# Another order of the sixteen column transfers of a band: 0, 4, 8, 12, 1, ... in place of 0, 8, 1, 9, ...

## The chip, the core and the metric

The kernel runs on one core of a Trainium2 chip. The core has TensorE (PE, matmuls, with its weight loads PEld), VectorE (DVE), ScalarE (ACT), GpSimd (POOL) and SyncE (SP), and 16 DMA engines that move data between HBM and the on-chip memory SBUF. POOL and SP issue the DMAs here. The metric is the device time of one execution in microseconds; less is better.

## The reference

Two layers on x of shape 32 x 256 x 32 x 32, float32.

```python
# layer 0: 3x3 convolution of the group-normalised x, with rounding to a 16-bit format
x = x + conv3x3_quantized(_gn(x), weight, bias)
# layer 1: involution of the group-normalised x
xn = _gn(x)
y = relu(bn(einsum('oc,bchw->bohw', w1, xn)))             # 256 -> 64 channels
w = einsum('oc,bchw->bohw', w2, y) + b2                   # 16 groups x 49 taps for each pixel
w = w.reshape(b, G, K * K, H, W)
patches = ...                                             # the 7x7 surroundings of each pixel of xn
x = x + einsum('bgkhw,bgckhw->bgchw', w, patches)         # each pixel has its own 7x7 filter per group
```

In layer 1 each pixel of each image has 16 x 49 weights of its own, worked out from the image, and the sum over its 7 x 7 surroundings uses them.

## The kernel before, in words

Images are worked through one after another, in a schedule written out by hand: a loop over steps n (line 549), 16 steps to an image (`per`, line 540). At each step every stage is asked, with its own lag, what is due (`due`, line 542), and issues it. The order of the code in the loop is the order of each engine's queue.

For an image, `front` (line 284) normalises, runs the convolution (line 332, TensorE), adds it to x, normalises again, makes y (line 380) and transposes the pixels (line 395). `weights` (line 402) makes the filter weights of four rows with matmuls (line 410) and VectorE puts them, with b2, into a ring `w_sb` (line 428).

The filters then have to change their place. A pixel's contributions go to its 7 x 7 surroundings, and the kernel does that sum as a matmul in which the contracted partitions are pixels. `scatter` (line 466) writes the ring to HBM, to the tensor `wd` of 32 rows x 38 columns x 1124 float32, with seven SP transfers for a band of eight image rows (line 477), in packets of 640 bytes. `load_bands` (line 479) reads the band back into SBUF, to one of three band tiles of 128 partitions x 2 sides x 3524 float32. Partition 16 r + j of a band holds row r (of 8) and column j (of 16) of each of the two sides of the image. Four bands make an image, 128 the whole run.

A band is loaded by sixteen transfers, one for each column j. Each goes to eight partitions (j, j + 16, ..., j + 112), for each of the two sides, with rows of 1124 float32 (4496 bytes): 16 such rows, 70.2 KB. In the loop over i from 0 to 15, j is worked out from i (line 483). Which queue issues it follows from i alone: i = 7 and i = 15 go to SP, the other fourteen to POOL (line 489). Inside one partition column j begins at j x 160 float32, so the transfers write disjoint places.

`sums` (line 501) multiplies the band with the pixels (line 515): each matmul takes 64 partitions, that is four rows with all sixteen columns. `add_windows` (line 523) adds the result to x with VectorE (line 531), and `store` (line 533) writes x to the output from SP. `load_bands` of a band is due 9 steps ahead of its `sums` (line 590).

The semaphores that the program uses let eight POOL transfers be out at once: each waits for the POOL transfer eight places before it. The first transfer of a band on each queue also waits for the scatters that wrote its rows of `wd` and for the matmuls that last read that band tile.

Of the kernel before, what the change touches and what calls it, by code (L numbers as in the profile page):

```python
# [41 lines left out]
JC = W // SIDES  # L42
# [29 lines left out]
def tile_quant_conv_then_involution(  # L72
# [406 lines left out]
    def load_bands(b, k):  # L479

        band = bands[(b * K + k) % NBAND]
        for i in range(JC):
            j = i // 2 + i % 2 * JC // 2
            src = bass.AP(
                tensor=wd.tensor,
                offset=wd.offset + k * TR * ROW + (j + PAD1) * WPIX,
                ap=[[ROW - 1, TR], [JC * WPIX, SIDES], [1, WPIX]],
            )
            queue = nc.sync if i % SHARE == SHARE - 1 else nc.gpsimd
            queue.dma_start(band[j::JC, :, j * WB : j * WB + WPIX], src)  # L490
# [51 lines left out]
    def due(n, lag):  # L542

        b, i = divmod(n - lag, per)
        return (b, i) if 0 <= b < B else (None, None)

    with tc.manual_schedule():
        fronts = {}
        for n in range(FRONT, B * per + 2):
            b, i = due(n, FRONT)  # L550
# [12 lines left out]
            b, i = due(n, 0)  # L563
            if b is not None and i % 2 == 0:
                sums(b, i // 2)
            b, i = due(n, 1)
# [6 lines left out]
            b, i = due(n, 2)  # L573
            if b is not None and i == 2 * (M - 1 - SIDES):
                store(b, 0)
            b, i = due(n, -LEAD)
# [3 lines left out]
            for part in range(2):  # L580
                b, i = due(n, -LEAD + 1 + part)
# [4 lines left out]
            b, i = due(n, LOAD)  # L586
# [3 lines left out]
            b, i = due(n, 3 - 4 * NBAND)  # L590
            if b is not None and i % 4 == 0:
                load_bands(b, i // 4)
# [37 lines left out]
```

## Time and profile before

| | |
|---|---|
| runs | 1381.25, 1392.44, 1393.82 us; median 1392.44 |
| span of the profiled execution, first to last instruction | 1387.9 us (its own time isn't recorded beside it; the median of the runs is 4.5 us more) |
| mean granted clock of TensorE | 0.981 |
| VectorE, ScalarE, POOL busy | 934.7, 727.6, 1007.6 us |
| POOL transfers of line 490 | 1792, 547 ns each to issue |
| SP transfers of line 490 | 256, 602 ns each to issue (median) |
| HBM read, written | 183.81 MB, 180.74 MB: 263 GB/s over the span |

How to read a profile here: an engine's busy time says how full it is, not whether it sets the end. A line such as `X L1 <- Y L2: a, n, m` in the waits says that X stood idle before line L1 for a us in all, n times, at most m us, and that Y's line L2 was the last to release it. The chain of work that ended last is followed back from the last instruction, at each step to what released it. DMA queue q0 is POOL's, q1 is SP's; their shares are the time of their packets over 16 engines' span.

### The profile page before, as it was taken

The page shows a single profiled execution, that of the slowest core. Times are in us where ns is not written, and L with a number is a line of the kernel's source. Part 1 is how long each engine was busy: PE and PEld are TensorE (multiplying, and loading weights), DVE is VectorE, ACT ScalarE, POOL GpSimd, SP SyncE. Part 2 cuts the span into 40 slices and gives each one's busy share as a digit, 9 for nine tenths or more (in the row PEclk, how much of TensorE's full clock was granted, in tenths as well). Part 3 has the DMA queues.
Part 4 walks back from the last instruction along what each step waited for, and adds up shares of the span by engine and source line. Part 5 has one row for each costly group of instructions (what it writes and reads, how often), then busy time and mean ns, then how long its engine had stood idle before and what let it go on. Part 6 is the DMA issues. An engine that isn't in the chain of part 4 may idle for free.

```text
span 1387.9 us, 70012 instructions
## 1 busy us (share of the span) xinstructions
PE 1250.5 (90%) x29440; PEld 798.5 (58%) x29440; DVE 934.7 (67%) x3179; ACT 727.6 (52%) x1699; POOL 1007.6 (73%) x1818
## 2 busy tenths in 40 slices
PE   2899999899899999998899999899999999999665
PEld 1356555566565665655565666566566655666543
DVE  4467776677767776776576677667777776677652
ACT  4866555465645555655455555545565654653300
POOL 8057777777787777767777787776876777778785
PEclk9999999999999999999999999999999999999986
DMA  6079999999999998999999999999999999999995
GB/s 217 1 195 286 283 277 283 284 266 292 287 277 274 287 294 254 285 279 269 273 275 286 289 275 279 288 277 264 288 283 272 295 285 279 280 280 272 280 269 162
DMA packets 366232, 369.33 MB, mean 266 GB/s; under 512 B 78624, under 2 KB 308192, under 8 KB 365664
## 3 DMA queue, kind: packets, MB, share of 16 engines
q1 hardware_dynamic: 279904, 235.72, 57.5%
q0 software_dynamic: 86016, 129.14, 33.8%
q8 instruction: 234, 3.83, 1.2%
q14 instruction: 78, 0.64, 0.1%
HBM read 183.81 MB, written 180.74 MB: 263 GB/s over the span
## 4 chain that ended last, share of the span: by engine, by line
PE 55%; DMA 25%; DVE 5%; issue 5%; POOL 4%; SPq 3%; ACT 3%; POOLq 0%; DVEq 0%; ACTq 0%
PE pc L332 22%; PE acc L515 17%; DMA band<-wd 14%; PE pw L410 10%; DMA wd<-w_sb 8%; POOL band L490 4%; PE py L380 3%; DVE w_sb L428 3%; SPq L477 3%; PE pt L395 2%; DMA out<-x 1%; ACT junk L219 1%; DVE x L531 1%; DMA band<-in_w 1%; ACT xn L278 0%
## 5 line engine op out<-in xcount | busy, mean ns | idle before, releaser
L490 POOL DMA_DIRECT2D band<-wd x1792 | 978.0, 548 | 364.1 <-DMA band<-wd 225.3
L428 DVE TENSOR_TENSOR w_sb<-pw,b_sb 128x16 f32<-128x16 f32 (+9 forms) x1920 | 455.5, 349 | 359.2 <-PE pw L410 345.4
L332 PE MATMUL pc<-xq,wq 128*128 128x496 f16 (+3 forms) x2304 | 536.4, 379 | 32.5 <-ACT xq L278 28.0
L515 PE MATMUL acc<-band,pixels 64*32 64x190 f32 (+1 forms) x16384 | 411.6, 322 | 80.2 <-DMA band<-wd 44.6
L332 PEld LDWEIGHTS <-wq 128*128 128x128 f16 x2304 | 206.8, 98 | 328.2 <-issue 113.0
L515 PEld LDWEIGHTS acc<-band,pixels 64*32 64x32 f32 x16384 | 296.1, 108 | 165.1 <-issue 100.1
L410 PE MATMUL pw<-w_sb,y 64*32 64x224 f32 (+1 forms) x8192 | 291.2, 332 | 15.1 <-issue 13.9
L531 DVE TENSOR_TENSOR x<-acc,x 128x380 f32<-128x380 f32 (+1 forms) x512 | 261.7, 511 | 33.6 <-PE acc L515 24.6
L410 PEld LDWEIGHTS pw<-w_sb,y 64*32 64x32 f32 x8192 | 180.6, 106 | 45.7 <-issue 28.8
L399 ACT COPY pixels<-pt 128x512 f32<-128x512 f32 x128 | 73.6, 575 | 224.0 <-PE pt L395 224.0
L219 ACT ACTIVATE junk<-x 128x512 f16<-128x512 f32 (+1 forms) x192 | 146.5, 763 | 18.0 <-DVE x L348 9.6
L219 ACT ACTIVATE junk<-x,mean 128x1024 f16<-128x1024 f32 x128 | 147.1, 1149 | 4.3
L250 ACT ACTIVATE s<-back,eps 128x2 f32<-128x2 f32 x64 | 18.9, 296 | 207.3 <-DVE back L235 207.2
L346 DVE TENSOR_SCALAR q<-pc 128x512 f16<-128x512 f32 x128 | 87.2, 682 | 19.2 <-PE pc L332 19.0
L278 ACT ACTIVATE xn<-x,off,rstd 128x512 f32<-128x512 f32 x128 | 96.1, 800 | 0.0
L348 DVE SCALAR_TENSOR_TENSOR x<-q,bias_sb,x 128x512 f32<-128x512 f16 x128 | 92.0, 719 | 0.2
L395 PEld LDWEIGHTS pt<-ident,xn 128*128 128x128 f32 x512 | 63.9, 142 | 27.7 <-issue 3.3
L395 PE MATMUL pt<-ident,xn 128*128 128x128 f32 x512 | 78.0, 275 | 1.5 <-ACT pixels L399 1.5
L240 ACT ACTIVATE mean<-back 128x2 f32<-128x2 f32 x64 | 12.7, 198 | 120.6 <-DVE back L235 120.6
L278 ACT ACTIVATE xq<-x,off,rstd 128x1024 f16<-128x1024 f32 x64 | 75.5, 1226 | 0.0
L380 PEld LDWEIGHTS py<-xn,w_sb 128*64 128x64 f32 x2048 | 62.7, 138 | 16.7 <-issue 8.3
L380 PE MATMUL py<-xn,w_sb 128*64 128x64 f32 x2048 | 67.5, 224 | 2.8 <-ACT xn L278 1.8
(40 smaller groups left out, 374.5 us busy)
## 6 DMA issues: line engine op xcount, KB each, us to landing
wd<-w_sb SPq DMA_DIRECT2D x896, 160.0 KB
band<-wd POOLq DMA_DIRECT2D x1792, 70.2 KB, 4.9
x<-in_x SPq DMA_DIRECT2D x64, 512.0 KB
out<-x SPq DMA_DIRECT2D x64, 512.0 KB
band<-wd SPq DMA_DIRECT2D x256, 70.2 KB
band<-in_w SPq DMA_DIRECT2D x2, 1152.0 KB
w_sb<-in_w SPq DMA_DIRECT2D x2, 196.0 KB
wd<-band SPq DMA_DIRECT2D x2, 180.0 KB
```

The source lines that it names most:

```text
L219: nc.scalar.activation(junk[:, n0:n1], src[:, h, n0:n1], func, bias=bias, accum_out=self.sums[:, i : i + 1])
L278: nc.scalar.activation(dst, src, AF.Identity, bias=self.off[:, one], scale=self.rstd[:, one])
L332: nc.tensor.matmul(pc.rearrange("p (r c) -> p r c", c=W)[:, r0 - nt * RT : r1 - nt * RT, c0:c1], wq[:, kh, k, mh * P : (mh + 1) * P], xq[: ...
L346: nc.vector.tensor_scalar(q, pc, F16_MAX, -F16_MAX, ALU.min, ALU.max)
L348: nc.vector.scalar_tensor_tensor(xt[:, mh, cols], q, bias_sb[:, mh : mh + 1], xt[:, mh, cols], ALU.add, ALU.add)
L380: nc.tensor.matmul(py[i * CR : (i + 1) * CR, cols], w1_sb[:, kh, :], px[:, r : r + 2], start=kh == 0, stop=kh == CH - 1,)
L395: nc.tensor.transpose(pt[:, i, h * P : (h + 1) * P], xn[:, h, (m + i) * P : (m + i + 1) * P], ident)
L410: nc.tensor.matmul(pws[i][t * TW : (t + 1) * TW, r, : dj.stop - dj.start], y_sb[b % 2][half, (r0 // 2 + r) * W : (r0 // 2 + r + 1) * W], w ...
L428: nc.vector.tensor_tensor(to, pws[i][:p, r : r + rows, e, d0 * G : d1 * G].rearrange("p r (d g) -> p r d g", g=G), b2_sb[:p, e, d0 * G : d ...
L490: queue.dma_start(band[j::JC, :, j * WB : j * WB + WPIX], src)
L515: nc.tensor.matmul(at[t * TW : (t + 1) * TW, h, :, f - top : l - top], px[p, a, v * GC : v * GC + TW], of[:, :, 2 * a + v, f - top : l - top],
L531: nc.vector.tensor_tensor(x_at, of, x_at, ALU.add)
```

## The change

In `load_bands` the column that is loaded at place i of the loop is another one. Before, the columns come in the order 0, 8, 1, 9, 2, 10, 3, 11, 4, 12, 5, 13, 6, 14, 7, 15. After, in the order 0, 4, 8, 12, 1, 5, 9, 13, 2, 6, 10, 14, 3, 7, 11, 15. The two that SP issues (i = 7 and 15) are columns 11 and 15 before and columns 13 and 15 after.

```diff
         band = bands[(b * K + k) % NBAND]
         for i in range(JC):
-            j = i // 2 + i % 2 * JC // 2
+            j = i % 4 * JC // 4 + i // 4
             src = bass.AP(
                 tensor=wd.tensor,
                 offset=wd.offset + k * TR * ROW + (j + PAD1) * WPIX,
```

## Prediction

> **What bounds the kernel now.** I read the page first: engine shares, queues, chain. Then five stretches of the steady part, then the waits, then what line 490 waits for.
>
> ```profile
> PE 1250.5 (90%) x29440; PEld 798.5 (58%) x29440; DVE 934.7 (67%) x3179; ACT 727.6 (52%) x1699; POOL 1007.6 (73%) x1818
> q1 hardware_dynamic: 279904, 235.72, 57.5%
> q0 software_dynamic: 86016, 129.14, 33.8%
> PE 55%; DMA 25%; DVE 5%; issue 5%; POOL 4%; SPq 3%; ACT 3%; POOLq 0%; DVEq 0%; ACTq 0%
> ```
>
> Two resources are nearly full: TensorE (90% of the span) and the 16 DMA engines (57.5 + 33.8 and 1.3 for instructions = 92.6%). The chain that ended last is 55% TensorE and 25% transfers. By stretches (columns: the stretch, its length, busy us of PE, PEld, DVE, ACT, POOL, each with its count, clock, DMA share, GB/s):
>
> ```profile
> 400.00:600.00 200.00, 190.66 (x4575) 122.05 (x4577) 141.41 (x482) 112.62 (x263) 151.82 (x279) 0.99 0.96 276
> 800.00:1000.00 200.00, 187.95 (x4488) 120.60 (x4487) 139.34 (x487) 112.22 (x262) 151.15 (x277) 0.99 0.97 278
> ```
>
> In the steady part TensorE is busy 94 to 95% of the time and the DMA engines 96 to 97%. A change in what one band packet costs could therefore reach the end. A change only in which packet comes first could not. The waits say how often TensorE stands for a band:
>
> ```profile
> DVE w_sb L428 <- PE pw L410: 345.4, 228, 5.9
> POOL band L490 <- DMA band<-wd: 225.3, 308, 2.9
> ...
> PE acc L515 <- DMA band<-wd: 44.6, 24, 5.6
> ```
>
> POOL stands 225.3 us, in 308 waits, for an earlier band transfer: each POOL transfer waits, by the semaphores of the program, for the POOL transfer eight before it, so eight are out at once. TensorE itself stands only 44.6 us for a band, in 24 waits (23.9 us in 17 of them between 200 and 1300 us). The transfers themselves:
>
> ```profile
> band<-wd POOLq DMA_DIRECT2D x1792, 70.2 KB, 4.9
> ...
> band<-wd SPq DMA_DIRECT2D x256, 70.2 KB
> ```
>
> [...] I call this the column's group, 0 to 3. The old order has groups 0, 2, 0, 2, 0, 2, 0, 2 and then 1, 3, 1, 3, 1, 3, 1, 3[...]. The new one has 0, 1, 2, 3 over and over. [...] The trace shows no engine numbers. [...] when SP's two are nearly alone (717.0 to 717.8 us) 5 to 8 of their packets are under way at once.
>
> **Does the trace show the groups?** I looked at the records of single packets, 4496 bytes each, 16 to a transfer. POOL's 28,672 have a median of 187 ns, a tenth percentile of 173 and a mean of 242.6; SP's 4,096 have a mean of 237. With 1 to 3 band packets under way (80 ns after a packet's start, no load of x beside it) the mean is 223 to 226 ns, with 6 to 8 it is 233 to 236, with 16 it is 286. So load costs something. The group does not, as far as I can see: SP's column 15 (group 3) takes 210 ns beside six or more POOL packets of the second half of a band (groups 1 and 3) and 279 beside those of the first half (0 and 2). SP's column 11 (group 2) takes 227 beside the first half, which has its own group, and 243 beside the second. [...] A fit of POOL's durations on same-group packets under way gives -0.6 +- 0.4 ns per packet, other groups +0.2 +- 0.4. Two reservations: I put packets to columns by their order of start, so neighbours can be confused; and the 279 comes from moments with much in flight at once, which load alone may explain.
>
> **The change, part by part.**
> 1. The value of j. It is worked out when the program is made; no instruction is added. Cost 0, with nothing needed to hide it.
> 2. Issues. Still 14 on POOL and 2 on SP for each of 128 bands, at 547 ns on POOL (1792 x 0.547 = 980 us, the 978.0 of the page) and 602 ns on SP. The queue follows i, not j, so nothing moves past anything on SP's or POOL's queue. SP's pair becomes columns 13 and 15 instead of 11 and 15. Cost 0.
> 3. Waits. The first transfer on each queue carries the waits for the scatters into wd and for the matmuls that read the band; these need all columns in either order. The limit of eight out goes by place in the queue too. No wait is added. Cost 0.
> 4. The reader. Each matmul of line 515 takes 64 partitions, four rows of all sixteen columns, so it needs the last landing of the sixteen; which column that is does not matter, and the first and the last place are columns 0 and 15 in both orders. Cost 0.
> 5. The packets. Bytes, lengths and number are the same: 147 MB in 32,768 packets, 2,048 for each of 16 engines. Only which SBUF partitions and which places of wd are touched together changes. This is the only term that can differ from zero. From below: [...] an engine would save 20 ns x 2,048 = 41 us. From above: if packets of one group met more often, see the slower rival, +25 us. I take 0, since the trace shows no dependence on the group and two bounds of either sign.
>
> The sum is 0 on a span of 1387.9 us. The median of the runs is 1392.4, that is 4.5 us more than this span, so I predict 1392 us. The three runs shown go from 1381 to 1394, so about 1% is what a measurement of this kernel can tell from no change.
>
> What covers a small cost: POOL needs 14 x 0.547 = 7.7 us for a band, and a band comes every (1374.2 - 81.5) / 128 = 10.1 us. Eight transfers out and 4.9 us to land make 0.61 us each, 8.6 us a band. Only when the median landing passes 10.1 / 14 x 8 = 5.8 us (+18%) does POOL's queue alone set the pace. If that cover is gone, sums of the next band are late first, then add_windows on VectorE and the store behind it.
>
> **Rivals.**
> *Faster[...].* For it: [...] DMA engines at 96 to 98% in the steady part, and the growth from 223 to 286 ns with the load. Against it: the same growth would come from HBM reads or the engines, the comparison by group goes the wrong way[...]. The engines would save up to 41 us, but TensorE can only give back its waits for a band: 24 us in the steady part. 1392 - 24 = 1368 us. It decides once packets get shorter by 24 / 2,048 us = 12 ns.
>
> *Slower[...].* [...] Say 2 of 7 packets go from 243 to the 286 ns seen with 16 under way: 2/7 x 43 = 12 ns, x 2,048 = 25 us on engines with 3% to spare. With no cover, 1392 + 25 = 1417 us. It decides from about 7 ns a packet (14 us, 1%). [...]
>
> *No effect because order is lost anyway.* With eight transfers out and engines shared with the scatter's 229,376 packets of 640 bytes, neighbours in the queue overlap in both orders; 1392 us too. It differs from the forecast in cause only.
>
> **How the numbers follow.** No difference of the packets, from either cause: 0.60, between 1381 and 1403 us. Faster rival: 0.15, down to 1368. Slower rival: 0.20, up to 1417. Something in wd's addresses that I can't price, slower: 0.05. So within 1%: 0.60, faster by over 1%: 0.15, slower: 0.25. The range from 1368 to 1417 takes in both bounds and leaves out less than 2 in 10; the likeliest case's own is 1381 to 1403.
>
> **What would show it.** Right: 1792 POOL issues at 547 ns, a landing near 4.9 us, q0 near 33.8%, POOL's wait for bands near 225 us, TensorE's for bands near 45. Faster rival: q0 below 33%, landing below 4.7 us, TensorE busy above 95% in the steady stretches. Slower rival: q0 above 35%, landing above 5.1 us, more of the chain on band<-wd. My forecast falls if the mean band packet changes by more than 7 to 12 ns, or if a wait of line 490 appears that was not there.

## The result, and the profile after

The changed kernel takes 1386.7 us (median of 20 runs) against 1393.9 us for the kernel before (20 runs beside it): ratio 0.9956, 95% interval 0.9935 to 0.9977. That is 0.4% faster, inside the 1% that the forecast called no difference. Run again later (e7 below) it came to 0.9984 (0.9963 to 1.0005), which does not exclude no change.

The page of the changed kernel, the lines that answer to those of before (engine shares, the two queues, the chain by engine):

```profile
PE 1259.7 (91%) x29440; PEld 798.8 (58%) x29440; DVE 928.0 (67%) x3179; ACT 728.1 (53%) x1699; POOL 1009.7 (73%) x1818
q1 hardware_dynamic: 279904, 235.72, 57.3%
q0 software_dynamic: 86016, 129.14, 33.7%
PE 65%; DMA 19%; issue 5%; POOL 4%; ACT 3%; DVE 2%; SPq 1%; POOLq 0%; DVEq 0%; ACTq 0%
```

Two of the steady stretches and the waits, as before:

```profile
400.00:600.00 200.00, 189.73 (x4532) 119.94 (x4516) 139.90 (x478) 111.91 (x258) 150.66 (x277) 1.00 0.97 281
800.00:1000.00 200.00, 192.34 (x4557) 122.21 (x4549) 143.36 (x513) 111.10 (x263) 152.62 (x281) 1.00 0.97 284
```

```profile
DVE w_sb L428 <- PE pw L410: 336.7, 228, 5.8
...
POOL band L490 <- DMA band<-wd: 216.6, 259, 3.3
...
PE acc L515 <- DMA band<-wd: 27.4, 15, 3.8
```

The shares of the two queues moved by 0.1 and 0.2 points, the DMA engines are as full as before (97% busy in both stretches, 96 and 97% before), POOL's wait fell by 9 us, and TensorE's wait for a band fell from 44.6 to 27.4 us. The last figure looks like the gain. It isn't safe: the same kernel profiled again in e7 shows 43.1 us there. The chain changed its shares too (DMA 25 to 19%), but in e7 DMA has 29%. Both differ more between two profiles of the changed kernel than between before and after. The lines of e7:

```profile
PE 51%; DMA 29%; POOL 5%; issue 5%; DVE 4%; ACT 3%; SPq 2%; POOLq 0%; DVEq 0%; ACTq 0%
```

```profile
POOL band L490 <- DMA band<-wd: 229.0, 288, 3.3
...
PE acc L515 <- DMA band<-wd: 43.1, 21, 6.2
```

Nor does the pair of profiled spans show the gain. Line 490 of each kernel, what the issues took and when the first and last started (before, then after):

```profile
L490 POOL DMA_DIRECT2D band<-wd x1792: 547/547/683, 81.5 to 1374.2; - x200
...
DMA to landing us min/median/max: 2.4/4.9/8.1
```

```profile
L490 POOL DMA_DIRECT2D band<-wd x1792: 547/547/681, 75.0 to 1371.4; - x200
...
DMA to landing us min/median/max: 2.4/4.9/8.8
```

The first band transfer starts 6.5 us earlier in the second profile, in the start-up where the order of columns plays no part yet. From the first to the last issue it is 1292.7 us before and 1296.4 us after. The span is 2.9 us shorter only for the start-up. A gain of 0.4% was to be had from many runs, not from one profile.

### The profile page after: what moved, and what is told of

It reads as the page before. It is cut to its first block, busy times and chain, and to the rows that moved or that the text cites. A ratio compares the mean times of both kernels' runs of the same rounds, so it can differ in the third digit from the quotient of the medians.

```text
span 1385.0 us, 70012 instructions
## 1 busy us (share of the span) xinstructions
PE 1259.7 (91%) x29440; PEld 798.8 (58%) x29440; DVE 928.0 (67%) x3179; ACT 728.1 (53%) x1699; POOL 1009.7 (73%) x1818
## 4 chain that ended last, share of the span: by engine, by line
PE 65%; DMA 19%; issue 5%; POOL 4%; ACT 3%; DVE 2%; SPq 1%; POOLq 0%; DVEq 0%; ACTq 0%
PE pc L332 27%; PE acc L515 20%; DMA band<-wd 13%; PE pw L410 12%; DMA wd<-w_sb 5%; POOL band L490 4%; PE py L380 3%; PE pt L395 3%; DVE w_sb L428 1%; SPq L477 1%; ACT junk L219 1%; DMA band<-in_w 1%; ACT xn L278 0%; ACT xq L278 0%; ACT rstd L271 0%
## 5 line engine op out<-in xcount | busy, mean ns | idle before, releaser
L515 PE MATMUL acc<-band,pixels 64*32 64x190 f32 (+1 forms) x16384 | 419.6, 322 | 67.8 <-issue 29.4
L219 ACT ACTIVATE junk<-x 128x512 f16<-128x512 f32 (+1 forms) x192 | 146.5, 763 | 18.6 <-DVE x L348 11.6
```

Of the source, the lines that this page charges most:

```text
L219: nc.scalar.activation(junk[:, n0:n1], src[:, h, n0:n1], func, bias=bias, accum_out=self.sums[:, i : i + 1])
L515: nc.tensor.matmul(at[t * TW : (t + 1) * TW, h, :, f - top : l - top], px[p, a, v * GC : v * GC + TW], of[:, :, 2 * a + v, f - top : l - top],
```

## The experiments

All are edits of the kernel before. Times are medians. The ratio, with its 95% interval, is that on record to runs of the kernel before on the same chip; it is not the quotient of the two medians and can differ from it by up to 0.2%. "Packet" is the mean duration of POOL's 28,672 band packets of 4496 bytes, worked out from the packet records of the profile (242.6 ns before, 242.2 after; other profiles of orders that cost no time lie between 244 and 251, so 5 ns there mean nothing). A column's group is j // 4, 0 to 3, here as in the prediction: columns 0 to 3 are group 0, columns 4 to 7 group 1, and so on. That columns belong together in these fours is the author's assumption; no run shows that the fours begin and end there.

**e1, columns in plain order.** Does the order matter at all? In POOL's queue columns of one group now follow each other, 0,0,0,0,1,1,1 and then 2,2,2,2,3,3,3.

```diff
-            j = i // 2 + i % 2 * JC // 2
+            j = i
```

> Columns 0, 1, 2, ..., 15 in plain order: [...] this is the worst order for groups, slower than before by 10 to 40 us, mean band packet above 255 ns. HBM theory (the gain comes from which places of wd are read together): neighbours in wd are now read together, slower or faster by over 5 us, I can't say which. No-packet theory (order of columns does not matter to packets, and the 6 us is something else): within 5 us of before, band packet 240 to 245 ns.

1485.6 us, ratio 1.0625 (1.0585 to 1.0665); packet 271.5 ns. The order matters much, and more than the 10 to 40 us that were expected of the worst order for groups. The view of line 490, POOL's and TensorE's waits for bands, and a steady stretch of e1:

```profile
DMA to landing us min/median/max: 2.7/5.5/8.5
```

```profile
POOL band L490 <- DMA band<-wd: 285.8, 384, 2.8
...
PE acc L515 <- DMA band<-wd: 86.4, 54, 6.3
```

```profile
800.00:1000.00 200.00, 178.83 (x4137) 115.30 (x4144) 129.21 (x434) 99.13 (x229) 139.32 (x255) 0.97 1.00 260
```

The DMA engines are busy without a gap (share 1.00), at 260 GB/s where the kernel before moves 278 in the same stretch. TensorE has lost 9 of 188 us to waiting. The median landing is 0.6 us later. The sum over all packets fits: packets longer by 28.9 ns (POOL's 28,672), 43.9 (SP's 4,096), 3.2 (the scatter's 229,376) and 12.3 (8,192 of the loads of x) are 115 us for each of 16 engines; the run is 89 us longer.

**e2 and e3, one half of the change each.** The partitions that are written (SBUF) and the columns of wd that are read (HBM) change separately. If what counts is which partitions are written together, e2 has the gain and e3 does not; if it is which places of wd are read together, the other way round.

```diff
+            jd = i % 4 * JC // 4 + i // 4
             src = bass.AP(
...
-            queue.dma_start(band[j::JC, :, j * WB : j * WB + WPIX], src)
+            queue.dma_start(band[jd::JC, :, jd * WB : jd * WB + WPIX], src)
```

That is e2; e3 gives j the new formula and jd the old one.

> The new order for the partitions that are written, the old order for the columns of wd that are read (the data of a column lands in another column's partitions, so the output is not the reference's; packets, sizes and waits are the same). [...] the whole gain, 5 to 7 us faster than before. HBM theory: as before within 3 us. No-packet theory: as before within 3 us.

> The other half: the old order for the partitions that are written, the new order for the columns of wd that are read (output not the reference's for the same reason). HBM theory: the whole gain, 5 to 7 us faster than before. [...] as before within 3 us. No-packet theory: as before within 3 us.

e2: 1394.2 us, 0.9983 (0.9965 to 1.0002). e3: 1396.0 us, 1.0002 (0.9979 to 1.0024). The HBM half shows nothing. The SBUF half leans the right way, but is not clear of zero: the effect is too small to be split like this, so I split the large one.

**e5 and e6, the two halves of the plain order.** As e2 and e3, with `jd = i` and the old j (e5), or `j = i` and the old jd (e6). If the side that is written counts, e5 has the loss and e6 is as before; if the side that is read, the reverse.

> The plain order 0, 1, 2, ... for the partitions that are written, the old order for the columns of wd that are read (output not the reference's). [...] nearly the whole loss of the plain order, 5 to 7% slower than before, mean POOL band packet 265 to 275 ns. HBM theory: as before within 0.5%, packet near 243 ns.

> The other half: the old order for the partitions that are written, the plain order for the columns of wd that are read (output not the reference's). [...] as before within 0.5%, packet near 243 ns. HBM theory: 5 to 7% slower, packet 265 to 275 ns.

e5: 1487.7 us, 1.0650 (1.0611 to 1.0690), packet 268.3 ns. e6: 1393.1 us, 0.9984 (0.9961 to 1.0008), packet 249.3 ns. POOL's and TensorE's waits for a band in e5, then in e6 (line numbers are one higher for the added line):

```profile
POOL band L491 <- DMA band<-wd: 305.0, 382, 3.2
...
PE acc L516 <- DMA band<-wd: 80.6, 47, 6.7
```

```profile
POOL band L491 <- DMA band<-wd: 226.6, 294, 3.0
...
PE acc L516 <- DMA band<-wd: 46.7, 19, 7.7
```

e5 has the waits of e1, e6 those of the kernel before. This settles the side: what counts is the side that is written, not which places of wd are read together. With a column's partitions its place inside the partition (j x 160 float32) moves too, in these runs and in those below, except in e13; that the partitions count and not this place is not shown apart.

**e4, e8 and e11, SP's pair.** In the change SP gets columns 13 and 15 in place of 11 and 15. e4 and e11 make this exchange alone, in the old order; e8 keeps the new order without it. If SP's pair makes the gain, e4 is faster by 5 to 7 us and e8 has lost it; if not, e4 is as before within 3 us.

```diff
+            j = {11: 13, 13: 11}.get(j, j)
```

> The old order with columns 11 and 13 exchanged, so that SP issues columns 13 and 15 as in the changed kernel, and POOL's order is else the old one. SP-pair theory [...]: 5 to 7 us faster than before. [...] as before within 3 us.

> The new order with columns 11 and 13 exchanged, so that SP issues columns 11 and 15 as before, and POOL's order is else the new one. SP-pair theory: the gain is gone, within 0.2% of before. Spread theory (POOL's new order brings the gain[...]): 0.3 to 0.7% faster than before, as the changed kernel.

> The old order with columns 11 and 13 exchanged, once more. If its 0.8% over before is real, 0.5 to 1.1% faster than before; if it was a chance of few runs, between 0.4% faster and 0.1% slower.

e4: 1386.1 us, 0.9923 (0.9885 to 0.9961) from seven runs. That looked like the whole gain. e11, the same kernel later, with 14 runs: 1393.6 us, 0.9981 (0.9958 to 1.0004). e8: 1393.1 us, 0.9972 (0.9952 to 0.9992); this ratio rests on 20 of its 22 runs, and the mean of all 22 is 0.9981 of before's. So the exchange alone has no gain that repeats: e4's large value, whose interval excluded 1, did not come again. And what there may be of a gain does not need the exchange.

**e7, the change once more.**

> The changed kernel once more, beside the next one on the same chip. If the measured gain is real: 0.3 to 0.7% faster than before. If it was chance or a property of one chip: within 0.2% of before.

1392.7 us, 0.9984 (0.9963 to 1.0005), less than was expected of a real gain and within what was allowed for chance; it does not exclude zero. The first measurement, 0.9956, and e8's 0.9972 do, so a gain of 0.2 to 0.4% may be there, but it is not shown: e6, which writes the partitions in the old order, came to 1393.1 us beside e7's 1392.7 and e8's 1393.1 on the same chip, with the ratio of e7, 0.9984.

**e9 and e10, neighbours of one group.** Why is the plain order bad and the old one good? The pair theory says that neighbours of one group in POOL's queue cost time. Take POOL's fourteen transfers of a band two by two, the first with the second, the third with the fourth. In the old and in the new order no such pair has the same group. In e1 five of seven pairs have it.

```diff
-            j = i // 2 + i % 2 * JC // 2
+            j = (0, 1, 8, 9, 2, 3, 10, 11, 4, 5, 6, 12, 13, 7, 14, 15)[i]
```

e10 has (0, 1, 8, 9, 4, 5, 12, 11, 13, 2, 3, 10, 14, 6, 7, 15).

> Order 0, 1, 8, 9, 2, 3, 10, 11, 4, 5, 6, 12, 13, 7, 14, 15; SP still issues columns 11 and 15. [...] now POOL's transfers two by two belong to the same group (0,0, 2,2, 0,0, 2,1, 1,1, 3,3, 1,3). Pair theory [...]: slower than before by 2 to 6%. Window theory (what counts is how many groups are among the eight transfers that are out): as before within 0.5%.

> Order 0, 1, 8, 9, 4, 5, 12, 11, 13, 2, 3, 10, 14, 6, 7, 15; SP still issues columns 11 and 15. POOL's transfers two by two belong to the same group, but all four groups come within eight transfers (0,0, 2,2, 1,1, 3,3, 0,0, 2,3, 1,1). Pair theory: slower than before by 1.5 to 6%. Window theory: as the changed kernel, 0.1 to 0.5% faster than before.

e9: 1439.0 us, 1.0302 (1.0264 to 1.0340), packet 257.4 ns. e10: 1416.1 us, 1.0133 (1.0089 to 1.0177), packet 255.7 ns. The view of line 490 of e9, and its waits, then those of e10:

```profile
DMA to landing us min/median/max: 2.6/5.2/8.6
```

```profile
POOL band L490 <- DMA band<-wd: 264.4, 355, 3.3
...
PE acc L515 <- DMA band<-wd: 58.8, 40, 7.1
```

```profile
POOL band L490 <- DMA band<-wd: 257.8, 352, 2.9
...
PE acc L515 <- DMA band<-wd: 48.7, 26, 4.9
```

The window theory by itself falls with e9, which has as many groups in a half band as the old order and loses 3%. The pair theory is right in sign for both, and e10 lies a little under the range it gave. Both seem to count: e10 has six pairs and loses less than e9 with five; what sets it apart is that all four groups come within eight transfers. So pairs together cost 3.0% where the queue mostly holds two groups (e9), and 1.3% where it holds four (e10). More groups among eight are worth 1.7% where pairs are together. Where they are apart, more groups are the change itself, and its gain is not clear of the scatter.

Two things stay open. Pairs don't explain e1, which has five as e9 has and loses twice as much. If every neighbour in POOL's queue is counted and not only pairs, 10 of 13 are of one group in e1 and 6 in e9 and in e10, which puts e1 in its place but not e9 above e10. And all neighbours of one group in e1, e9 and e10 are also neighbouring columns (0 and 1, 8 and 9). An order that puts 0 beside 2 or 3 (one group, columns apart) or 3 beside 4 (two groups, columns together) would tell the group from plain nearness; it was not run.

**e13, other partitions for a column.** Does what is left of the slow packets come from which partitions are written together? Each column goes here to eight partitions four apart in place of sixteen apart. If it does come from there, the packets and the time should fall (215 to 230 ns, 0.5 to 2% faster); if not, both stay (240 to 250 ns, within 0.4%).

```diff
-            queue.dma_start(band[j::JC, :, j * WB : j * WB + WPIX], src)
+            p0 = j % 4 + j // 4 * 32
+            queue.dma_start(band[p0 : p0 + 29 : 4, :, j * WB : j * WB + WPIX], src)
```

> The old order of columns, but column j goes to partitions p0, p0 + 4, ..., p0 + 28 with p0 = j % 4 + 32 (j // 4), in place of j, j + 16, ..., j + 112 (the rows of pixels and band no longer match, so the output is not the reference's; packets and sizes are the same; since a column now lies in one half of the partitions, the waits between the transfers and the matmuls come apart by halves, which can ease them a little). [...] mean POOL packet 215 to 230 ns, 0.5 to 2% faster than before. [...] packet 240 to 250 ns, as before within 0.4%.

1383.4 us, 0.9892 (0.9859 to 0.9925). The time is that of the first case, but POOL's mean packet, 244.4 ns, is that of the second. SP's fell from 237 to 220 ns. By load: with 16 band packets under way the mean is 212 ns (286 before, 262 after the change, 330 in e1); with 1 to 3 under way it is 232 (225, 227 and 239). The figures for 16 under way are thin: about 1% of the band packets have 16 under way, and e7, the changed kernel again, has 235 there. With 13 to 15 under way, a tenth of the packets, the mean is 241, against 263 before and 254 in e7. Of POOL's packets 18.6% take over 280 ns, against 19.7% before. So the packets are shorter where very many are under way, and the rest stays as it was. This layout leaves most of the slow packets of the kernel before as they were; what makes them it doesn't show. How much of the 1.1% is the partitions written together and how much is the waits that came apart by halves, this run can't say. With this layout a half of the partitions no longer holds four rows of all columns, which the matmuls of line 515 need, so it is no version of the kernel; a layout that has both was not tried.

## Why the prediction was right, and where its reason was wrong

- The time, no difference within 1% and centred on 1392 us, held: 1386.7 us, 0.4% under.
- Steps 1 to 4 (nothing added, no queue or wait changed, same reader) held: 1792 issues at 547 ns, median landing 4.9 us, in both profiles.
- That the sum came out near 0 was luck in part. The same five steps, applied to the plain order, would have given 0 as well, and e1 is 6.3% slower.
- Step 5 held in its result for another reason than the one given. "The group does not [cost something], as far as I can see" was wrong: e1 and e5 put 6.3 and 6.5% on the order in which the partitions are written, with the same bytes, queues and rules of waiting, and e9 and e10 tie it to the groups of neighbours. The reading failed for two reasons. In the kernel before, a POOL packet has on average 5.0 packets of its group under way beside it, but 4.9 of them belong to its own transfer and only 0.2 to another (1.2 in e1), so there was little to compare. And the reading was too coarse: the same fit on the packet records of e1, where the cost is there, gives +2.1 +- 0.4 ns for a packet of the same group and +3.6 +- 0.5 for one of another, so it doesn't see the group there either. A trace of a kernel that avoids a cost can't show that the cost is absent.
- The right reason for a small effect: the old order already keeps neighbours in different groups, which avoids the 3 to 6% of e9 and e1. The change only adds groups to the eight that are out.
- The cover was not where the prediction looked for it. It let POOL's queue set the pace from a median landing of 5.8 us on; e9 lost 41 us at 5.2 and e1 89 us at 5.5, with the DMA engines busy without a gap in e1 (shares of 0.99 to 1.01 in the five stretches).
- The slower rival had a cost (packets that meet others of their group) and applied it to the wrong order: the new one is not slower (0.9956, 0.9984) and its packets are not longer (242.2 ns against 242.6). That 2 of 7 packets would meet in it was the author's assumption; no trace shows it. The price, 43 ns (286 with 16 under way less 243), came to 12 ns with 2 of 7; by the same estimate the 5 of 7 pairs of e1 and e9 would give 31. The packets of e1 are 29 ns longer and those of e9 15. Which DMA engine carries a packet is not shown; the records have no engine numbers. That neighbours in the queue should differ is shown by e9 (1.0302), and the runs in which the partitions written change their order agree with the grouping by j // 4, though no run tells it from neighbouring columns.
- The faster rival may have had the right sign, but of its 24 us at most 7 came (1386.7 against 1393.9 at first, 1392.7 against 1397.4 in e7), and even these are not sure. That its packets would be up to 20 ns shorter was an estimate from the 243 and 223 ns of the trace before; they came out 0.4 ns shorter.
- Two readings were off without harm. The stretch in which SP's packets are nearly alone is 705.7 to 706.5 us on the clock of the profile's span, not 717.0 to 717.8. And over all five stretches TensorE is busy 93 to 96% of the time, not 94 to 95, and the DMA engines 96 to 98%.

Open: whether the change gains anything, and where in the profile it would show (waits and packets of e7 differ from those of the first profile by more than the effect); whether the group or the nearness of columns makes neighbours in the queue costly; and what makes the 20% of packets over 280 ns.

## What to carry to other kernels

Where many small transfers that each reach only a few partitions are out at once, try an order in which neighbours in the queue go to partitions that lie apart; here neighbours of different j // 4 avoided the 6% that the plain order cost (ratio 1.0625, e1) on engines that were 97% busy. Once neighbours differed, further spreading was worth at most a few tenths of a per cent (0.9956 and 0.9984). To judge such a term, run the case that pays the cost: a trace of the good order doesn't contain it.

## What was not expected of the hardware

- Order on the HBM side did nothing: reading wd's neighbouring columns together (e6) gave 0.9984 (0.9961 to 1.0008).
- The plain order of the partitions written also lengthened packets that don't write SBUF: the scatter's 640-byte packets, from SBUF to HBM, took 39.3 ns in e1 and 39.6 in e5, against 36.1 before and in e6. That is 46 of the 115 us by which each engine's packets grew (3.2 ns x 229,376 / 16).
